# A graph network layer on one core: the selector's product in four instructions of three tiles

## The chip, the core and the metric

The kernel runs on one core of a Trainium2 chip. A core has five engines with an instruction stream each: PE (matrix products), DVE (vector), ACT (scalar), POOL (general, here the issuer of gathers) and SP (here the issuer of most plain loads). The metric is the device time of one execution in microseconds (us). The median of 16 executions of the kernel before is 4510.51 us, the lowest 4504.17, the highest 4518.46.

## The reference

There are 12500 nodes of 160 numbers (64 scalars, and 32 vectors of three components) and 400000 edges, sorted by their destination. Cut to what matters, with `a` the node attribute and the scale factors left in:

```python
h = jnp.maximum(_layernorm(x, axis=-1), 0.0)
y0 = x0 @ W_l1_0 * a * inv0
y1 = jnp.einsum('nuc,uv->nvc', x1, W_l1_1) * a[:, :, None] * inv1
w = jax.nn.silu(edge_length_embedded @ fc_W1 * ...) @ fc_W2 * ...      # 192 weights for each edge
ys0 = y0[edge_src]
ys1 = y1[edge_src]
e0 = edge_attr[:, :1]
e1 = edge_attr[:, 1:]
mid_a = w_a * ys0 * e0
mid_d = w_d * jnp.einsum('euc,ec->eu', ys1, e1) * (1.0 / math.sqrt(3.0))
mid_b = (w_b * ys0)[:, :, None] * e1[:, None, :]
mid_c = (w_c * e0)[:, :, None] * ys1
z0 = zeros.at[edge_dst].add(concatenate([mid_a, mid_d]))
z1 = zeros.at[edge_dst].add(concatenate([mid_b, mid_c]))
out0 = C_S * s0 + C_X * (z0 @ W_l2_0 * ...)
out1 = C_S * s1 + C_X * (einsum(z1, W_l2_1) * ...)
return x + concatenate([out0, out1])
```

`edge_attr` is called e4 in the kernel: its first number is `e0`, and the other three are its vector part `e1`. The product with the vector part in `mid_b` is where the change lies.

## The kernel before

**Stages.** First the node stage normalizes the nodes, multiplies them by the first weights, keeps the part `s` in `acc` on the chip and writes the part `y` to the table `y_d` in HBM. Then the edge loop runs, from about 284 us to 4443 us of the profile. Last comes a short stage that adds `acc` to `x` and writes the output. A loop for edges that are far from their window stands between; it is not entered with these inputs.

**Units of the edge loop.** An edge tile is 128 edges, one on each partition; there are 3125. A block is 4 tiles (`GT`), so there are 782 blocks. Three tiles make a window (`WT`): since the edges are sorted, their destinations are taken to lie among 32 neighbouring nodes (`WN`). Four windows are a group (`GW`) of 12 tiles (`TG`), which is 3 blocks; there are 261 groups, the last one with 5 tiles.

**What is done for a block.**
- `load(b)` issues, from POOL, one indirect DMA for each tile (L310): it takes a column of 128 node numbers from `src_sb`, in SBUF, and gathers those rows of `y_d` into `yg`. There are 10 buffers of `yg`, and loads are issued 8 blocks ahead (`AHEAD`). The edge attributes for the weights come in as `xe`, by SP.
- `hidden_pair` (L319, L324) and `weigh` (L341, L262, L263) make the edge weights `wt`, on PE and ACT.
- `products(b)` calls `multiply` on DVE: L268 multiplies the vectors of `yg` by `e1` into `tmp`, L270 reduces them to scalar products, and L271, L272, L273 and L275 write the 256 columns of `pr`. L268 is the first that needs `yg`, and so waits for the gathers.
- `sums(b)` on PE (L385) multiplies a selector by `pr` and adds the three tiles of a window in PSUM; ACT brings the result to SBUF (L390, L392).

**The selector.** `select(g)` builds, on DVE, the tile `sel` for the 12 tiles of a group: 128 partitions x 12 tiles x 4 planes x 32 nodes. Plane 3 is 1 where the edge's destination is that node (L364, from `iota` and `drel`). Planes 0 to 2 are plane 3 times the components of `e1` (L366, from `sel` and `ev`), so that one matrix product sums the scalar part and the three parts of `mid_b`. All of these operands are in SBUF. There are three buffers of `sel`.

**The end of a group.** `turn`, `linear` and `add` (L400, L409, L421) transpose the group's sums, multiply them by the last weights and place them with the help of `place` (L413, DVE); `accumulate` (L429, DVE) adds them to `acc`.

**The order.** The order of PE, ACT and DVE is written out by hand, and is kept. In turn b, DVE gets the products of block b+1, then at the last block of a group the accumulation of the group before, or at the middle block the selector of the next group:

```python
                if b + 1 < NB:
                    products(b + 1)
                if g and k == K - 1:
                    accumulate(g - 1)
                if k == 1 and g + 1 < NG:
                    select(g + 1)
                sums(b)
```

So the selector of a group is made a block or more ahead of the sums that use it. The first one is made before the loop.

Of the kernel before, what the change touches and what calls it, by code (L numbers as in the profile page):

```python
# [13 lines left out]
ALU = mybir.AluOpType  # L14
# [4 lines left out]
P = 128  # L19
# [10 lines left out]
WN = 32  # L30
WT = 3
# [10 lines left out]
def kernel(  # L42
# [19 lines left out]
    nc = tc.nc  # L62
# [214 lines left out]
    with (  # L277
# [68 lines left out]
        def e4_group(g):  # L346
            if g // EG not in ev4:
                lo, hi = g // EG * EG * TG, min((g // EG + 1) * EG * TG, TP)
                ev = ld.tile([P, EG * TG, 4], F32, name="ev")
                nc.sync.dma_start(ev[:, :hi - lo, :].rearrange("p t c -> p (t c)"), e4[:, lo * 4:hi * 4])  # L350
                ev4[g // EG] = ev
            return ev4[g // EG][:, g % EG * TG:(g % EG + 1) * TG, :]
# [5 lines left out]
        def select(g):  # L358

            ev = e4_group(g)  # L360
            lo, hi = g * TG, min((g + 1) * TG, T)
            n = hi - lo
            sel = selp.tile([P, TG, 4, WN], F32, name="sel")
            nc.vector.tensor_tensor(sel[:, :n, 3, :], iota[:, 0:WN].unsqueeze(1).to_broadcast([P, n, WN]),  # L364
                                    drel[:, lo:hi].unsqueeze(2).to_broadcast([P, n, WN]), ALU.is_equal)
            nc.vector.tensor_tensor(sel[:, :n, 0:3, :], sel[:, :n, 3:4, :].to_broadcast([P, n, 3, WN]),  # L366
                                    ev[:, :n, 1:4].unsqueeze(3).to_broadcast([P, n, 3, WN]), ALU.mult)
            sels[g] = sel

        def products(b):  # L370
# [64 lines left out]
        with order:  # L435
            for b in range(min(AHEAD, NB)):
                load(b)
            select(0)
            hidden_pair(0)
            weigh(0)  # L440
            if NB > 1:
                weigh(1)
            products(0)
            for b in range(NB):
                g, k = divmod(b, K)
                if b + AHEAD < NB:
                    load(b + AHEAD)
                if b + 2 < NB:
                    weigh(b + 2)
                if g:  # L450
                    (turn, linear, add)[k](g - 1)
# [7 lines that stand above are left out]
                if b % 4 == 0 and b + 4 < NB:  # L459
                    hidden_pair((b + 4) // 2)  # L460
            for h in ([NG - 2] if NG > 1 else []) + [NG - 1]:
                for k, stage in enumerate((turn, linear, add, accumulate)):
                    if h == NG - 1 or min(k, K - 1) > (NB - 1) % K:
                        stage(h)
# [4 lines left out]
    with (  # L469
# [10 lines left out]
        n = nc.values_load(far_i[0:1, 0:1], min_val=0, max_val=1)  # L480
        with tc.For_i(0, n, 1) as _:  # L481
            with tc.For_i(0, ZR, P) as r:
                nc.sync.dma_start(z_d[ds(r, P), :], zero)
            with tc.For_i(0, TP // GT, 1) as g:
                xe = fp.tile([FC_IN, 512], F32, name="f_xe")
                nc.sync.dma_start(xe, e16[ds(g * FC_IN, FC_IN), :])
                ev = fp.tile([P, GT, 4], F32, name="f_ev")
# [28 lines left out]
                for k in range(GT):  # L516
                    pd = fpp.tile([P, P], F32, name="f_pd")
                    nc.tensor.transpose(pd, df[:, k:k + 1].to_broadcast([P, P]), ident)
                    sel = fp.tile([P, P], F32, name="f_sel")
                    nc.vector.tensor_scalar(sel, pd, df[:, k:k + 1], None, ALU.is_equal)  # L520
                    m = fp.tile([P, ZC], F32, name="f_m")
# [87 lines left out]
```

## Time and profile before

| what | value |
|---|---|
| median of 16 executions | 4510.51 us |
| the profiled execution | 4510.26 us, of which the span from first to last instruction is 4508.4 |
| granted PE clock, mean | 0.92 |
| PE, DVE, ACT, POOL busy | 79%, 62%, 57%, 71% of the span |
| gathers, L310 on POOL | 3125 instructions, 3207.1 us busy, mean 1026 ns |
| the selector's product, L366 on DVE | 261 instructions, 353.7 us busy, mean 1355 ns |
| the selector's comparison, L364 on DVE | 261 instructions, 142.6 us busy, mean 546 ns |
| HBM | 307.62 MB read, 16.00 MB written |

The profile comes from one execution. A row such as "L366 DVE TENSOR_TENSOR sel<-sel,ev" names the line of the kernel, the engine, the operation, and what is written and read. Rows of the timeline give the start in us from the first instruction, the length in us, and in brackets the idle time of the engine ahead of it and what ended it. Consecutive DVE instructions can overlap by a little. "issue" as the end of an idle time means that no wait is seen there.

### The profile page before, as it was taken

What the parts mean: (1) busy time and instruction counts of PE and PEld (TensorE: products, weight loads), DVE (VectorE), ACT (ScalarE), POOL (GpSimd) and SP (SyncE); (2) the same over time, 40 slices, a digit from 0 to 9 for tenths busy, and PEclk for the clock granted to TensorE, in tenths of its full rate; (3) what the DMA queues carried; (4) which work ended last, traced back from release to release, by engine and by line L of the source; (5) the groups of instructions that cost most, each with busy time, mean ns of one, the idle gap of its engine ahead of it and who ended that gap; (6) DMA issues with size and microseconds to landing.
All of it is one profiled execution on the core that took longest, in us unless ns stands there. A gap on an engine that the chain in (4) does not pass through costs nothing. (4 is left out here: it accounts for less than half of the span.)

```text
span 4508.4 us, 60313 instructions
## 1 busy us (share of the span) xinstructions
PE 3541.9 (79%) x17263; PEld 2455.2 (54%) x17263; DVE 2796.5 (62%) x6412; ACT 2567.4 (57%) x9298; POOL 3215.0 (71%) x3135
## 2 busy tenths in 40 slices
PE   4887778878777878877788878877888778788773
PEld 3555555555555555555555555555555555555552
DVE  6656666666666666666666666666666666666664
ACT  1245655655565556555655555655655565555555
POOL 0037777777777777777777777777777777777773
PEclk9999998899999989899988898999999999989997
DMA  2222222222222222222222222222222222222225
GB/s 82 71 61 71 71 69 70 71 69 71 70 71 71 69 69 72 70 71 72 69 71 71 69 69 72 70 71 69 71 71 71 68 71 69 71 71 68 71 67 170
DMA packets 245943, 327.78 MB, mean 73 GB/s; under 512 B 66040, under 2 KB 195352, under 8 KB 245352
## 3 DMA queue, kind: packets, MB, share of 16 engines
q0 software_dynamic: 150000, 256.20, 21.5%
q1 hardware_dynamic: 81030, 59.43, 4.4%
q10 hardware_dynamic: 14578, 8.25, 0.6%
q8 instruction: 141, 2.31, 0.2%
q14 instruction: 194, 1.59, 0.1%
HBM read 307.62 MB, written 16.00 MB: 72 GB/s over the span
## 5 line engine op out<-in xcount | busy, mean ns | idle before, releaser
L310 POOL DMA_INDIRECT yg<-y_d,src_sb x3125 | 3207.1, 1026 | 1187.8 <-issue 914.0
L385 PE MATMUL pz<-pr,sel 128*128 128x256 f32 x6250 | 1710.4, 422 | 680.1 <-DVE pr L275 678.7
L385 PEld LDWEIGHTS pz<-pr,sel 128*128 128x128 f32 x6250 | 1246.3, 209 | 953.5 <-DVE pr L275 528.6
L268 DVE TENSOR_TENSOR tmp<-yg,ev 128x384 f32<-128x384 f32 x782 | 436.6, 558 | 1523.5 <-DMA yg<-y_d,src_sb 1520.3
L262 ACT ACTIVATE wt<-pw,ev 128x96 f32<-128x96 f32 x3125 | 808.5, 344 | 326.4 <-ACT zs L392 212.1
L390 ACT ACTIVATE zs<-pz 32x192 f32<-32x192 f32 x1042 | 337.0, 323 | 1005.5 <-PE pz L385 996.6
L341 PE MATMUL pw<-w,hT 64*128 64x192 f32 x6250 | 780.2, 371 | 0.2 <-ACT wt L263 0.2
L341 PEld LDWEIGHTS pw<-w,hT 64*128 64x128 f32 x6250 | 533.4, 201 | 393.4 <-issue 392.4
L392 ACT ACTIVATE zs<-pz 32x64 f32<-32x64 f32 x3126 | 667.6, 214 | 41.5
L270 DVE TENSOR_REDUCE tmp<-tmp 128x128 f32<-128x384 f32 x782 | 463.8, 593 | 27.1
L319 PE MATMUL px<-xe,w 32*128 32x512 f32 x782 | 338.3, 710 | 144.6 <-DVE acc L429 143.2
L273 DVE TENSOR_TENSOR pr<-wt,yg 128x384 f32<-128x384 f32 x782 | 429.1, 549 | 0.0
L324 ACT ACTIVATE hT<-px 128x512 f32<-128x512 f32 x391 | 219.3, 595 | 328.1 <-PE px L319 324.9
L263 ACT ACTIVATE wt<-pw 128x384 f32<-128x384 f32 x782 | 398.8, 510 | 0.0
L366 DVE TENSOR_TENSOR sel<-sel,ev 128x1152 f32<-128x1152 f32 (+1 forms) x261 | 353.7, 1355 | 14.2 <-DMA ev<-in_e 5.3
L271 DVE TENSOR_TENSOR pr<-wt,yg 128x256 f32<-128x256 f32 x782 | 334.1, 427 | 0.0
L272 DVE TENSOR_TENSOR pr<-wt,yg 128x256 f32<-128x256 f32 x782 | 324.7, 415 | 0.0
L409 PE MATMUL px<-wo,za 128*128 128x160 f32 x1566 | 285.6, 319 | 0.4 <-ACT za L402 0.4
L409 PEld LDWEIGHTS px<-wo,za 128*128 128x128 f32 x1566 | 222.7, 191 | 62.2 <-ACT zs L392 33.0
L319 PEld LDWEIGHTS px<-xe,w 32*128 32x128 f32 x782 | 88.2, 204 | 275.5 <-DVE acc L429 198.3
L275 DVE TENSOR_TENSOR pr<-wt,tmp 128x128 f32<-128x128 f32 x782 | 219.9, 281 | 0.0
L421 PE MATMUL px<-os,place 128*128 128x160 f32 x1044 | 212.9, 327 | 0.4 <-ACT os L411 0.4
(78 smaller groups left out, 1733.5 us busy)
## 6 DMA issues: line engine op xcount, KB each, us to landing
yg<-y_d,src_sb POOLq DMA_INDIRECT x3125
xe<-in_e SPq DMA_DIRECT2D x784, 32.0 KB
xt<-in_x SPq DMA_DIRECT2D x26, 560.0 KB
y_d<-yb SPq DMA_DIRECT2D x13, 560.0 KB
out<-xt ACTq DMA_DIRECT2D x13, 560.0 KB
ev<-in_e SPq DMA_DIRECT2D x32, 192.0 KB
src_sb<-in_src SPq DMA_DIRECT2D x1, 1568.0 KB
dst_i<-in_dst SPq DMA_DIRECT2D x1, 1568.0 KB
```

The lines of the kernel that those rows point to most:

```text
L262: nc.scalar.activation(wt[:, k, 0:96], pw[:, k, 0:96], AF.Copy, scale=ev[:, k, 0:1])
L263: nc.scalar.activation(wt[:, :n, 96:NW], pw[:, :n, 96:NW], AF.Copy)
L268: nc.vector.tensor_tensor(tmp[:, :n, 0:3, :], y1, ev[:, :n, 1:4].unsqueeze(3).to_broadcast([P, n, 3, M1]), ALU.mult)
L270: nc.vector.tensor_reduce(tmp[:, :n, 3, :], tmp[:, :n, 0:3, :].rearrange("p t c u -> p t u c"), AX.X, ALU.add)
L273: nc.vector.tensor_mul(pr[:, :n, 96:192].rearrange("p t (c u) -> p t c u", c=3), wt[:, :n, M0:96].unsqueeze(2).to_broadcast([P, n, 3, M1]) ...
L310: nc.gpsimd.indirect_dma_start(out=yg[:, k, :], out_offset=None, in_=y_d, in_offset=bass.IndirectOffsetOnAxis(ap=src_sb[:, t:t + 1], axis=0))
L319: nc.tensor.matmul(ph, w1[r, :], xe[r, :], start=True, stop=True)
L341: nc.tensor.matmul(pw[:, k, 0:NW], hT[r, o:o + P], w2[r, :], start=True, stop=True)
L366: nc.vector.tensor_tensor(sel[:, :n, 0:3, :], sel[:, :n, 3:4, :].to_broadcast([P, n, 3, WN]), ev[:, :n, 1:4].unsqueeze(3).to_broadcast([P, ...
L385: nc.tensor.matmul(pz[:, 0:PC], sels[g][:, t % TG, :, :], pr[:, k, :], start=t % WT == 0, stop=last)
L392: nc.scalar.activation(zs[:, 192 + M0 * c:192 + M0 * (c + 1)], pz[WN * c:WN * (c + 1), 192:PC], AF.Copy)
L409: nc.tensor.matmul(po[:m, :], za[:, k, :m], wo[:, k, :], start=k == 0, stop=k == 2)
```

## The change

`select` multiplies by the vector part of e4 in pieces of `WT` = 3 tiles, one window each. A group of 12 tiles takes four instructions of 128 x 288 elements in place of one of 128 x 1152; the last group, of 5 tiles, takes two. What is computed, the tiles, their buffers and the place of `select` in the order are as before.

```diff
             nc.vector.tensor_tensor(sel[:, :n, 3, :], iota[:, 0:WN].unsqueeze(1).to_broadcast([P, n, WN]),
                                     drel[:, lo:hi].unsqueeze(2).to_broadcast([P, n, WN]), ALU.is_equal)
-            nc.vector.tensor_tensor(sel[:, :n, 0:3, :], sel[:, :n, 3:4, :].to_broadcast([P, n, 3, WN]),
-                                    ev[:, :n, 1:4].unsqueeze(3).to_broadcast([P, n, 3, WN]), ALU.mult)
+            for t in range(0, n, WT):
+                m = min(WT, n - t)
+                nc.vector.tensor_tensor(sel[:, t:t + m, 0:3, :], sel[:, t:t + m, 3:4, :].to_broadcast([P, m, 3, WN]),
+                                        ev[:, t:t + m, 1:4].unsqueeze(3).to_broadcast([P, m, 3, WN]), ALU.mult)
             sels[g] = sel
```

## The prediction

> **What bounds the kernel now.** I read the page's busy shares first, then its costliest groups. The columns of a group are busy time, mean ns of one, idle time of the engine before, and what ended that idle time.
>
> ```profile
> PE 3541.9 (79%) x17263; PEld 2455.2 (54%) x17263; DVE 2796.5 (62%) x6412; ACT 2567.4 (57%) x9298; POOL 3215.0 (71%) x3135
> L310 POOL DMA_INDIRECT yg<-y_d,src_sb x3125 | 3207.1, 1026 | 1187.8 <-issue 914.0 <-DMA xe<-in_e 236.0 <-DMA yg<-y_d,src_sb 21.6
> ...
> L268 DVE TENSOR_TENSOR tmp<-yg,ev 128x384 f32<-128x384 f32 x782 | 436.6, 558 | 1523.5 <-DMA yg<-y_d,src_sb 1520.3
> ...
> L366 DVE TENSOR_TENSOR sel<-sel,ev 128x1152 f32<-128x1152 f32 (+1 forms) x261 | 353.7, 1355 | 14.2 <-DMA ev<-in_e 5.3
> ```
>
> PE has the largest busy share, yet it is not the bound. DVE waits 1520.3 us for gathers (L268), and PE waits 678.7 us for DVE's `pr`. The gathers are issued by POOL, one instruction per edge tile. Does POOL wait for anybody? The view of the waits, POOL alone, with total us, times, longest:
>
> ```profile
> POOL yg L310 <- issue: 914.0, 3000, 0.3
> POOL yg L310 <- DMA xe<-in_e: 236.0, 1, 236.0
> POOL yg L310 <- DMA yg<-y_d,src_sb: 21.6, 71, 0.3
> ```
>
> After the start-up wait of 236.0 us no pause is longer than 0.3 us, whatever name is beside it: that is POOL's fixed step between two issues. So from 283.7 us (first issue) to 4442.6 us (end of the last) POOL runs without a break, and the whole time is 283.7 + the sum of 3125 issues + a tail of 66 us. Only the length of an issue can change it. An undisturbed one takes 946 ns (the median of L310), with the step 1.25 us; the mean is 1026. The excess, 3125 x 80 ns = 250 us, is time on the path. Where does it come from? The timeline around one call of `select`, DVE rows and then POOL rows (start us, length us):
>
> ```profile
> 2012.18 0.28 DVE L275 TENSOR_TENSOR pr<-wt,tmp 128x128 f32<-128x128 f32 x1
> 2012.38 0.55 DVE L364 TENSOR_TENSOR sel<-iota,drel 128x384 f32<-128x384 f32 x1
> 2012.96 1.36 DVE L366 TENSOR_TENSOR sel<-sel,ev 128x1152 f32<-128x1152 f32 x1
> 2014.97 0.56 DVE L268 TENSOR_TENSOR tmp<-yg,ev 128x384 f32<-128x384 f32 x1 [0.65 <-DMA yg<-y_d,src_sb]
> 2015.56 0.59 DVE L270 TENSOR_REDUCE tmp<-tmp 128x128 f32<-128x384 f32 x1
> ...
> 2010.99 0.94 POOL L310 DMA_INDIRECT yg<-y_d,src_sb  x1 [0.30 <-issue]
> 2012.24 1.04 POOL L310 DMA_INDIRECT yg<-y_d,src_sb  x1 [0.30 <-issue]
> 2013.58 1.55 POOL L310 DMA_INDIRECT yg<-y_d,src_sb  x1 [0.30 <-issue]
> 2015.44 0.95 POOL L310 DMA_INDIRECT yg<-y_d,src_sb  x1 [0.30 <-issue]
> ```
>
> The issue at 2013.58 ends at 2015.13, which is 0.81 us after L366 ended (2014.32). The one at 2012.24 ends at 2013.28, 0.82 after L275 ended (2012.46). The issue at 2015.44 has its start inside L270, a reduction with one input, and is not lengthened. So some 0.135 us after its start (946 - 810 ns) an issue needs something that a DVE instruction with two SBUF inputs holds; it gets it when that instruction ends, and needs 0.81 us more. I applied this to all 3125 L310 rows: a lengthened row's end less 0.81 us falls within 30 ns of the end of a DVE instruction. By the DVE line released from: L366 145 us (one issue in almost every call of `select`, 0.56 us each), L275 31, L273 26, L271 26, L268 12, L364 7, L272 5. L366, the longest instruction of the loop, makes more than half of POOL's loss.
>
> **The change part by part.** What matters most is whether POOL gets through between two DVE instructions that follow each other at once. The trace has it, at L271 and L272 (two inputs each, the second started before the first ended):
>
> ```profile
> 2048.91 0.41 DVE L271 TENSOR_TENSOR pr<-wt,yg 128x256 f32<-128x256 f32 x1
> 2049.24 0.42 DVE L272 TENSOR_TENSOR pr<-wt,yg 128x256 f32<-128x256 f32 x1
> ...
> 2049.02 1.12 POOL L310 DMA_INDIRECT yg<-y_d,src_sb  x1 [0.30 <-issue]
> ```
>
> 2049.02 + 1.12 - 0.81 = 2049.33, the end of L271 and not of L272. In all lengthened rows of the trace no instruction ended between the point of need and the release: POOL is always let in at the first end.
>
> *Removed and added on DVE.* L366 has two sizes in the trace: 1152 elements 1358 ns, 480 elements 658 ns (its last call), so 1.042 ns per element and 158 ns fixed. A piece of 3 x 3 x 32 = 288 elements is then 458 ns. Independent instructions in a row overlap by 80 ns (L271 of 415 ns, L272 starts 335 ns later), so pieces start 378 ns apart and end at 458, 836, 1214 and 1592 ns. The four take 1592 ns against 1358: +234 ns x 260 = 61 us of DVE time. [...] The trace decides where that lies: DVE idles 0.65 us before the next L268 here, 1520.3 us in all, and L366's consumer, PE's L385, has no wait for `sel` in the list. So I cost it at nothing. Without that idle time L268 would be 0.23 us late, which delays PE's `pr` and still not POOL, whose buffers are free long before.
>
> *What POOL gains.* The point of need lies, after the start of L366: at about 0.75 us in 160 calls, 0.55 in 52, 1.20 to 1.34 in 48; in 16 rows at 0.08 POOL came first and was not held. With piece ends as above: at 0.75 held until 0.84, 0.09 us x 160 = 14 us; at 0.55 until 0.84, 0.29 x 52 = 15; of the late ones some 11 wait 0.27 for the last piece, 3 us, the others meet a seam; the early ones may now wait up to 0.37, 0 to 6 us. After a release the next need comes 1.25 us later, past the last piece. So 145 us shrink to 32 to 38: a gain of 109 us, end to end.
>
> *What moves.* POOL now arrives 0.4 us earlier in the block after `select`. In the rows above its next need was at 15.58, in L270, which holds nothing. 0.47 us earlier it is at 15.11, on the edge of L268 (held from 0.15 after its start), and the need after it at 16.36 falls into L271, 0.13 us. If it fell early into L268 it would cost up to 0.4. In the present trace that block loses 34 us in all, 0.13 per call, the other two 0.14 and, without L366, 0.15. Bounds: nothing (0.13 is already paid) or even 10 us gained, to 0.25 x 260 = 65 us lost. I take 17 us, near the low end, since three kinds of block with different phases all lose about 0.14.
>
> The L310 rows show the effect; what is held is unseen. [...]
>
> Sum: -109 + 17 = -92 us. The profiled execution took 4510.26 us (span 4508.4 and 1.9 around it), the median is 4510.51, so the sum stands against either: 4418 us.
>
> **The rivals.**
> *1 (0.79). As above*, 4418, its own range 4378 to 4458.
> *2 (0.07). No way in between the pieces:* if four instructions of one kind to one tile hand over without a seam, a need in any piece waits for the last. POOL then loses 0.234 us more per call: 260 x 0.234 = 61, 4571 us, slower. It decides if the release comes at 1592 ns and not at a piece's end; above 1358 ns the change loses. For it: pieces are alike and closer than the mixed lines of `multiply`. Against: L271, L272 and L273 are alike too, and release one by one.
> *3 (0.11). The gain is given back:* the earlier phase meets L268 (up to 0.4 us) and L271 (up to 0.3) in the next block in most calls. 0.3 x 260 = 78 lost, gain 31: 4480. For it: phases are locked, so a bad one repeats 260 times. Against: the present phases differ by block and lose alike.
> *4 (0.03). Another engine takes over, or the pieces wait for each other's end*: PE busy is 79%, and a group of 12 tiles shortens only from 15.9 to 15.5 us, so PE stays covered. With such waits the pieces start about 0.49 us apart, `select` grows 0.6 us and eats the 0.65 idle: 4505 to 4515.
>
> **How the numbers follow.** A measurement here tells about 0.2%, 9 us, from no change. Faster: 1 and nearly all of 3, 0.90; the same: 4 and a little of 3, 0.03; slower: 2, 0.07. The range takes in 1 with its unknown phase cost (up to 65 us lost, 10 gained, and the residue between 15 and 40) and half of 3: 4373 to 4470.
>
> **What would show it.** L366 with 1042 rows of about 458 ns, starts 0.38 apart; L310 still 3125 with a mean near 996 ns and pauses of 0.3; no L310 row over 1.4 us; idle before L268 still some 1450 us. A mean over 1026 proves 2; a mean near 1015, with more rows released from L268 and L271, proves 3; a pause of POOL over 0.3 us proves another bound.

## The result and the profile after

The changed kernel takes 4415.66 us (median of 8 executions, 4412.20 to 4421.21) against 4510.51 before. The ratio is 0.979, with a 95% interval of 0.9782 to 0.9798: 95 us faster. In a later set of runs, beside other experiments, it took 4406.61 against 4522.46 us, a ratio of 0.9739 (0.9723 to 0.9755): 116 us. The profiled execution after has a span of 4415.6 us at a granted PE clock of 0.92, as before. The selector's product is now line L368; lines behind it have moved by two.

The page's busy shares and the groups that answer to those shown of before:

```profile
PE 3520.6 (80%) x17263; PEld 2447.5 (55%) x17263; DVE 2850.7 (65%) x7193; ACT 2574.4 (58%) x9298; POOL 3124.1 (71%) x3135
...
L310 POOL DMA_INDIRECT yg<-y_d,src_sb x3125 | 3116.2, 997 | 1188.2 <-issue 901.7
...
L268 DVE TENSOR_TENSOR tmp<-yg,ev 128x384 f32<-128x384 f32 x782 | 436.4, 558 | 1378.4 <-DMA yg<-y_d,src_sb 1371.7
...
L368 DVE TENSOR_TENSOR sel<-sel,ev 128x288 f32<-128x288 f32 x1042 | 408.0, 453 | 14.3 <-DMA ev<-in_e 5.4
```

DVE has 781 instructions and 54 us of work more than before, and the kernel is faster. POOL has the same 3125 gathers and 91 us less work (3207.1 to 3116.2), with the same idle time (1187.8 to 1188.2). The waits of POOL say that it still runs without a break after the start (us in total, times, longest):

```profile
POOL yg L310 <- issue: 901.7, 2959, 0.3
POOL yg L310 <- DMA xe<-in_e: 236.2, 1, 236.2
POOL yg L310 <- DMA yg<-y_d,src_sb: 29.0, 95, 0.3
```

So the 91 us are the shorter issues. The timeline around one `select` shows how, DVE rows and then POOL rows (start us, length us; the four pieces are merged into one row):

```profile
2020.44 0.28 DVE L275 TENSOR_TENSOR pr<-wt,tmp 128x128 f32<-128x128 f32 x1
2020.64 0.55 DVE L364 TENSOR_TENSOR sel<-iota,drel 128x384 f32<-128x384 f32 x1
2021.22 1.56 DVE L368 TENSOR_TENSOR sel<-sel,ev 128x288 f32<-128x288 f32 x4
2023.22 0.56 DVE L268 TENSOR_TENSOR tmp<-yg,ev 128x384 f32<-128x384 f32 x1 [0.43 <-DMA yg<-y_d,src_sb]
2023.81 0.59 DVE L270 TENSOR_REDUCE tmp<-tmp 128x128 f32<-128x384 f32 x1
2024.32 0.41 DVE L271 TENSOR_TENSOR pr<-wt,yg 128x256 f32<-128x256 f32 x1
...
2020.51 1.03 POOL L310 DMA_INDIRECT yg<-y_d,src_sb  x1 [0.30 <-issue]
2021.85 1.02 POOL L310 DMA_INDIRECT yg<-y_d,src_sb  x1 [0.31 <-issue]
2023.17 0.95 POOL L310 DMA_INDIRECT yg<-y_d,src_sb  x1 [0.30 <-issue]
2024.43 1.13 POOL L310 DMA_INDIRECT yg<-y_d,src_sb  x1 [0.30 <-issue]
```

The issue at 2021.85 ends at 2022.87; less 0.81 that is 2022.06, the end of the second piece (pieces start 0.37 us apart and take 0.45, so the second ends at 2022.04). It took 1.02 us where the one in the same place took 1.55 before. The last POOL row shows the price: at 2024.43 the need falls into L271 and waits for its end at 2024.73.

The same reading of all L310 rows (excess over an undisturbed issue of about 945 ns, put down to the DVE line at whose end the row was released), in us, for six executions. The three light ones, with most of PE's work left out, come in the experiments:

| kernel | at the selector's product | at the other lines | sum | span | span less sum |
|---|---|---|---|---|---|
| before | 145.1 | 110.3 | 255.4 | 4508.4 | 4253.0 |
| changed | 28.6 | 135.4 | 164.0 | 4415.6 | 4251.6 |
| changed, later run | 42.2 | 112.4 | 154.6 | 4407.9 | 4253.3 |
| light, one piece | 170.9 | 92.8 | 263.7 | 4515.2 | 4251.5 |
| light, four pieces | 31.6 | 98.6 | 130.2 | 4382.2 | 4252.0 |
| light, twelve pieces | 27.3 | 140.2 | 167.5 | 4418.7 | 4251.2 |

The last column is constant to 2 us: the span is a fixed 4252 us plus the lengthening of POOL's issues, in all six. That accounts for the whole gain. In each of these executions the first issue of all takes 1.30 us and matches no DVE instruction; it stands under the other lines.

### The profile page after: what moved, and what is told of

It reads as the page before. It is cut to its first block, busy times and chain, and to the rows that moved or that the text cites. A ratio compares the mean times of both kernels' runs of the same rounds, so it can differ in the third digit from the quotient of the medians.

```text
span 4415.6 us, 61094 instructions
## 1 busy us (share of the span) xinstructions
PE 3520.6 (80%) x17263; PEld 2447.5 (55%) x17263; DVE 2850.7 (65%) x7193; ACT 2574.4 (58%) x9298; POOL 3124.1 (71%) x3135
## 3 DMA queue, kind: packets, MB, share of 16 engines
q8 instruction: 141, 2.31, 0.2%
## 5 line engine op out<-in xcount | busy, mean ns | idle before, releaser
L310 POOL DMA_INDIRECT yg<-y_d,src_sb x3125 | 3116.2, 997 | 1188.2 <-issue 901.7
L268 DVE TENSOR_TENSOR tmp<-yg,ev 128x384 f32<-128x384 f32 x782 | 436.4, 558 | 1378.4 <-DMA yg<-y_d,src_sb 1371.7
L270 DVE TENSOR_REDUCE tmp<-tmp 128x128 f32<-128x384 f32 x782 | 463.9, 593 | 27.1
L273 DVE TENSOR_TENSOR pr<-wt,yg 128x384 f32<-128x384 f32 x782 | 428.6, 548 | 0.0
L368 DVE TENSOR_TENSOR sel<-sel,ev 128x288 f32<-128x288 f32 x1042 | 408.0, 453 | 14.3 <-DMA ev<-in_e 5.4
L263 ACT ACTIVATE wt<-pw 128x384 f32<-128x384 f32 x782 | 399.2, 510 | 0.0
L271 DVE TENSOR_TENSOR pr<-wt,yg 128x256 f32<-128x256 f32 x782 | 335.2, 429 | 0.0
L272 DVE TENSOR_TENSOR pr<-wt,yg 128x256 f32<-128x256 f32 x782 | 324.6, 415 | 0.0
L275 DVE TENSOR_TENSOR pr<-wt,tmp 128x128 f32<-128x128 f32 x782 | 220.0, 281 | 0.0
```

Of the source, the lines that this page charges most:

```text
L263: nc.scalar.activation(wt[:, :n, 96:NW], pw[:, :n, 96:NW], AF.Copy)
L268: nc.vector.tensor_tensor(tmp[:, :n, 0:3, :], y1, ev[:, :n, 1:4].unsqueeze(3).to_broadcast([P, n, 3, M1]), ALU.mult)
L270: nc.vector.tensor_reduce(tmp[:, :n, 3, :], tmp[:, :n, 0:3, :].rearrange("p t c u -> p t u c"), AX.X, ALU.add)
L273: nc.vector.tensor_mul(pr[:, :n, 96:192].rearrange("p t (c u) -> p t c u", c=3), wt[:, :n, M0:96].unsqueeze(2).to_broadcast([P, n, 3, M1]) ...
L310: nc.gpsimd.indirect_dma_start(out=yg[:, k, :], out_offset=None, in_=y_d, in_offset=bass.IndirectOffsetOnAxis(ap=src_sb[:, t:t + 1], axis=0))
L368: nc.vector.tensor_tensor(sel[:, t:t + m, 0:3, :], sel[:, t:t + m, 3:4, :].to_broadcast([P, m, 3, WN]), ev[:, t:t + m, 1:4].unsqueeze(3).t ...
```

## The experiments

The first three groups of kernels ran on chips that granted PE a clock of 0.80 to 0.82 instead of 0.92; there the kernel before took 5450 and 5338 us. In every kernel traced there POOL stood idle ahead of L310 for 1750 to 2254 us, against 1188 in the kernel before at 0.92, so its issues alone no longer set the time. Their times can't test the theory. The rows of their traces can, since an undisturbed issue (median 946 to 949 ns) and a DVE instruction (L270, 593 ns in the mean before and with two pieces) have the same lengths there.

**Two, six and twelve pieces.** The edit is the step of the loop:

```diff
-            for t in range(0, n, WT):
-                m = min(WT, n - t)
+            for t in range(0, n, 6):
+                m = min(6, n - t)
```

and 2 or 1 in place of 6.

> Two pieces of six tiles. Theory (POOL is let in at the end of the first two-input instruction, so what counts is where in the pieces its need falls): pieces of 576 elements take 758 ns, start 678 ns apart and end at 0.76 and 1.44 us. The most frequent need, 0.75 us after the start, meets the seam and loses about 0.01 us; the needs at 0.55 lose 0.2, the late ones 0.1 to 0.24. POOL loses 20 to 35 us at this line in place of 145, and the time is 4400 to 4430 us, about that of four pieces. Rival (the loss goes with the length of one instruction): half of 145, some 72 us at this line, 4450 to 4465 us.

> Six pieces of two tiles. Theory of the seams: pieces of 192 elements take 358 ns, start 278 ns apart, ends at 0.36, 0.64, 0.91, 1.19, 1.47 and 1.75 us. Needs at 0.75 now wait 0.17 us (160 x 0.17 = 27 us), those at 0.55 wait 0.1: 30 to 40 us at this line, 4405 to 4435 us, no better than four pieces although the pieces are shorter. Rival (the loss goes with the length of one instruction): 20 to 25 us at this line, 4395 to 4408 us.

> Twelve pieces of one tile. Theory: pieces of 96 elements take 258 ns and start 178 ns apart; no need waits over 0.12 us, and some calls have two needs in their 2.2 us: 15 to 25 us at this line. DVE takes 0.6 us more per call than with four pieces, which is more than the 0.43 us that it idles before the next L268, but POOL waits for nothing of DVE's: 4395 to 4425 us. Rival (DVE's added time comes onto the path once its idle time behind the selector is used up): 0.2 to 0.4 us x 260 slower than four pieces, 4465 us or more.

Measured against the kernel before on the same chip: two pieces 1.0093 (1.0062 to 1.0125), six 1.0166 (1.0124 to 1.0207), twelve 0.9837 (0.9796 to 0.9878). Two pieces were run once more, with the same expected loss, on a second chip that again granted 0.82: 1.005 (1.0023 to 1.0078). None of the expected times came. The waits of POOL with two pieces say why:

```profile
DVE pr L271 <- ACT wt L263: 1204.1, 259, 40.5
POOL yg L310 <- DVE pr L275: 1043.1, 233, 11.7
POOL yg L310 <- issue: 847.7, 2768, 1.7
POOL yg L310 <- DMA xe<-in_e: 236.4, 1, 236.4
```

POOL now has breaks of up to 11.7 us until `multiply` is through with a block, which gives a buffer of `yg` back, and DVE in turn waits for ACT's weights. What sets the pace behind them was not followed to its end. The granted clock of PE differs too. Here are 200 us of the loop, first in the kernel before, at a granted clock of 0.92, then with two pieces here, at 0.77 (busy us of PE, PEld, DVE, ACT, POOL, with the number of instructions; granted clock; DMA share; GB/s):

```profile
2000.00:2200.00 200.00, 158.44 (x793) 109.80 (x795) 124.94 (x277) 116.99 (x426) 153.71 (x152) 0.92 0.26 71
...
2000.00:2200.00 200.00, 142.54 (x633) 100.17 (x635) 96.66 (x225) 96.74 (x348) 119.68 (x119) 0.77 0.21 56
```

POOL has 119 instructions in place of 152 in the same time. No trace of the kernel before at the low clock was kept. The rows say more than the times. With two pieces POOL lost 42.8 us at the product (42.7 in the second run), more than the 20 to 35 expected, and far from half of 145. With six it lost 15.9, less than the 30 to 40 that I expected from the phase. Since the phases differ on this chip, this doesn't separate "the phase decides" from "the length decides". In both, every row held at the product was released at the first end of a piece. With twelve pieces they were not:

```profile
385.67 2.11 DVE L368 TENSOR_TENSOR sel<-sel,ev 128x96 f32<-128x96 f32 x12
387.70 0.55 DVE L268 TENSOR_TENSOR tmp<-yg,ev 128x384 f32<-128x384 f32 x1
...
386.76 2.31 POOL L310 DMA_INDIRECT yg<-y_d,src_sb  x1 [0.30 <-issue]
```

386.76 + 2.31 - 0.81 = 388.26, the end of L268 (388.25): six pieces ended in between and POOL was not let in. 256 rows were passed over at one to six pieces, and lost 298 us. The rival of the prediction in which pieces hand over without a seam does exist, for pieces of 96 elements, though not for 192, 288 or 576.

Elsewhere a seam was missed with longer instructions too. From the run of two pieces, at L415 (a comparison of `iota` with one number per partition, which builds `place`):

```profile
400.98 0.35 DVE L415 TENSOR_SCALAR place<-iota,at 128x256 f32<-128x256 f32 x1
401.24 0.55 DVE L268 TENSOR_TENSOR tmp<-yg,ev 128x384 f32<-128x384 f32 x1
...
401.13 1.48 POOL L310 DMA_INDIRECT yg<-y_d,src_sb  x1 [1.21 <-DVE pr L275]
```

The need at 401.27 lies inside L415, which ends at 401.33, but 401.13 + 1.48 - 0.81 = 401.80 is the end of L268. Such rows number 97 with two pieces and 107 with six, and lost 52 and 57 us.

**One SBUF input.** What holds POOL up, a long instruction or one with two SBUF inputs? In the kernel before, the product is replaced by a reduction of the same size:

```diff
-            nc.vector.tensor_tensor(sel[:, :n, 0:3, :], sel[:, :n, 3:4, :].to_broadcast([P, n, 3, WN]),
-                                    ev[:, :n, 1:4].unsqueeze(3).to_broadcast([P, n, 3, WN]), ALU.mult)
+            nc.vector.tensor_reduce(sel[:, :n, 0:3, :], sel[:, :n, 3:4, :].to_broadcast([P, n, 3, WN]).unsqueeze(4),
+                                    AX.X, ALU.add)
```

> The selector's product as one instruction of the same 1152 elements, but a reduction over an axis of one, which has a single SBUF input: planes 0 to 2 become copies of plane 3, and the multiplication by e1 is left out. Theory (two SBUF inputs hold what POOL needs): an instruction of about 1.3 us that holds nothing, 0 us lost at this line, and 4385 to 4410 us with the phase given back. Rival (any long DVE instruction holds POOL up): 4500 to 4515 us as before.

> The selector's product as one instruction of the same 1152 elements with a single SBUF input (a reduction over an axis of one): planes 0 to 2 become copies of plane 3, and the multiplication by e1 is left out. Where PE is granted about 0.92: theory (two SBUF inputs hold what POOL needs) 0 us lost at this line, 4385 to 4410 us after the phase has given back 20 to 35. Rival (any long DVE instruction holds POOL up): 4500 to 4515 us. Where PE is granted about 0.80, POOL waits for buffers and no theory expects a gain in time.

> The same single-input product (the multiplication by e1 is left out) in four pieces of three tiles. It takes the number of instructions apart from what they hold: DVE has some 0.2 us more per call, about 55 us in all, and POOL loses nothing at this line either way. Theory (DVE's time is hidden in its wait for gathers): within 10 us of the single instruction with one input. Rival (more instructions cost time by themselves): 50 to 60 us slower than it.

Both runs of the single instruction were on chips with the low clock, and slower than before there: 1.018 (1.0142 to 1.0218) and 1.0175 (1.0095 to 1.0256); four pieces of it 1.0242 (1.0169 to 1.0316). The times say nothing for or against at this clock. The rows decide:

```profile
1908.41 1.35 DVE L366 TENSOR_REDUCE sel<-sel 128x1152 f32<-128x1152 f32 x1
1909.68 0.55 DVE L268 TENSOR_TENSOR tmp<-yg,ev 128x384 f32<-128x384 f32 x1
...
1909.50 0.94 POOL L310 DMA_INDIRECT yg<-y_d,src_sb  x1 [0.30 <-issue]
1910.74 0.95 POOL L310 DMA_INDIRECT yg<-y_d,src_sb  x1 [0.30 <-issue]
```

The issue at 1909.50 has its point of need, 0.135 us later, inside a DVE instruction as long as the one of before, and takes 0.94 us. In the first run 207 issues had their need inside L366 (at least 0.15 us after its start and over 0.02 us before its end), in the second 196: none took over 0.96 us, and the sum lost was under 0.1 us. In the kernel before it was 252 issues and 145 us. So it isn't the length of an instruction alone. The operation has changed too, from a product to a reduction; the next experiment keeps it.

**One of two inputs from PSUM.** The changed kernel, with L271 and L275 reading the weights where PE left them:

```diff
-        nc.scalar.activation(wt[:, :n, 96:NW], pw[:, :n, 96:NW], AF.Copy)
...
+        if all:
+            nc.scalar.activation(wt[:, :n, 96:NW], pw[:, :n, 96:NW], AF.Copy)
...
-        nc.vector.tensor_mul(pr[:, :n, 192:PC], wt[:, :n, 96:160], yg[:, :n, 0:M0])
+        w = wt if pw is None else pw
+        nc.vector.tensor_mul(pr[:, :n, 192:PC], w[:, :n, 96:160], yg[:, :n, 0:M0])
...
-        nc.vector.tensor_mul(pr[:, :n, M0:96], wt[:, :n, 160:NW], tmp[:, :n, 3, :])
+        nc.vector.tensor_mul(pr[:, :n, M0:96], w[:, :n, 160:NW], tmp[:, :n, 3, :])
```

In the edge loop `all` is False and `w` is `pw`, the tile in PSUM. L263 and its work fall away.

> The changed kernel, with L271 and L275 reading the edge weights straight from PSUM, so that they have one SBUF input each; ACT's copy of these weights (L263, 399 us busy) falls away. Theory: the 46 and 34 us that POOL loses at these two lines in the changed kernel go, some 10 to 30 come back at other lines by the phase: 4345 to 4390 us. Rivals: the operand from PSUM holds POOL up all the same, 4405 to 4425 us; PSUM is kept longer and PE's next weights come late, over 4425 us.

Again at the low clock: 1.016 (1.0086 to 1.0233). No expected time can be judged. The rows are the cleanest control of all, because operation and size are those of L271 in the changed kernel, and only one operand has moved (the line is L273 here, and the gather is L312):

```profile
2518.24 0.41 DVE L273 TENSOR_TENSOR pr<-pw,yg 128x256 f32<-128x256 f32 x1
...
2518.36 0.95 POOL L312 DMA_INDIRECT yg<-y_d,src_sb  x1 [0.30 <-issue]
```

The need at 2518.50 lies inside L273, and the issue takes 0.95 us. 146 issues had their need inside L273 by the same count, none over 0.96 us; in the changed kernel it was 267 inside L271, of which 208 were held, 46 us (the other 59 had it no later than 0.163 us after its start). So it is the second operand in SBUF that makes POOL wait for this product. It isn't the only form that does: in this run 157 issues with their need some 0.06 us before the end of L417 (the comparison that builds `place`, of one array with one number per partition) were released at its end. What in it holds POOL was not tried. In the run of two pieces, issues in the same position went past the end of this comparison to the end of L268; what tells the two apart is open. Whether this version would win at the clock of 0.92 wasn't run.

**The light kernels, on a chip that granted the kernel before 0.92.** To take PE out of the question, most of its work is left out, in the kernels with one, four and twelve pieces:

```diff
-            hT = hids[b // 2]
-            pw = p_w.tile([P, GT, 256], F32, name="pw")
+            if b < 2:
+                pws[b] = p_w.tile([P, GT, 256], F32, name="pw")
+            pw = pws[b % 2]
...
-                nc.tensor.matmul(pz[:, 0:PC], sels[g][:, t % TG, :, :], pr[:, k, :], start=t % WT == 0, stop=last)
+                if last:
+                    nc.tensor.matmul(pz[:, 0:PC], sels[g][:, t % TG, :, :], pr[:, k, :], start=True, stop=True)
...
-                if b % 4 == 0 and b + 4 < NB:
-                    hidden_pair((b + 4) // 2)
```

> The kernel before with little PE work: the edge weights come from the first two blocks only (L319, L324 and L341 run once for them, ACT still scales for every block), and L385 multiplies the last tile of each window alone. DVE's and POOL's work is whole. Theory (POOL's issues set the time, PE none of it): POOL without a break, 130 to 150 us lost at L366, 4480 to 4530 us on a chip of any clock. Rival (PE sets the time): well under 4400 us where PE is granted 0.92, and far under the 5340 to 5450 of the whole kernel where it is granted 0.80, with breaks of POOL left.

> The changed kernel with the same PE work left out as in l_one. Theory: 20 to 45 us lost at the four pieces, 80 to 115 us less than l_one. Rivals: no way in between the pieces, 40 to 70 us more than l_one; given back at other lines, less than 40 us less.

> Twelve pieces of one tile, with the same PE work left out as in l_one. First theory (let in at every piece's end): 60 to 130 us less than l_one. Theory after the run of twelve pieces in the whole kernel, where needs at the sixth piece and later were met only at the end of the next L268: POOL is not let in between pieces of 96 elements, most calls lose 0.7 us or more, and the time is 60 to 300 us more than l_one.

> The changed kernel as it is, beside the others on this chip. Where PE is granted about 0.92: 4405 to 4425 us, ratio 0.979. Where it is granted about 0.80, POOL waits for buffers that PE frees late, and what POOL saves is waited off: between the same and 2% slower than before, as with two and six pieces; POOL's loss at the pieces is still 20 to 60 us.

Measured: one piece 4509.23 us, four 4388.90, twelve 4423.11, and the whole changed kernel 4406.61 beside 4522.46 of before. With one piece PE's instructions fell from 17263 to 6085 and the time by 13 us: PE was not the bound. POOL lost 170.9 us at the product there, more than the 130 to 150 expected. Four pieces gained 120 us, a little above the 80 to 115 expected. The whole changed kernel came inside its expected 4405 to 4425 us, but its ratio of 0.9739 is a larger gain than the expected 0.979. What was expected of it at 0.80 did not come up; in the run of two pieces POOL's breaks at that clock ended with DVE's L275 (1043.1 us), and that PE frees the buffers late was not shown. The L310 rows of the light kernels, one piece and then four:

```profile
L311 POOL DMA_INDIRECT yg<-y_d,src_sb x3125 | 3215.5, 1029 | 1187.9 <-issue 937.1 <-DMA xe<-in_e 236.2 <-DMA yg<-y_d,src_sb 7.3
...
L311 POOL DMA_INDIRECT yg<-y_d,src_sb x3125 | 3082.2, 986 | 1188.2 <-issue 930.4 <-DMA xe<-in_e 236.1 <-DMA yg<-y_d,src_sb 10.1
```

133 us less POOL work, and the spans of these two executions differ by 133 us (4515.2 and 4382.2). Twelve pieces were 86 us faster than one and 34 slower than four, so the first expectation held for the time and the second did not, although its mechanism is in the trace: 69 rows were passed over at one or more seams and lost 45 us, against 256 and 298 us in the whole kernel at the low clock. Why fewer rows were passed over here is open: L268 followed the pieces with hardly any idle time in 217 of 261 calls here too. The run shows once more that PE doesn't set the time. Its PE clock in tenths over the span, after that of four pieces:

```profile
PEclk9999999999999999999999999999999999999997
...
PEclk9985555555555555555555555555555555555555
```

PE was granted half its clock nearly throughout (0.53 in the mean, against 0.99 with four pieces), and the span was still 4251 us plus POOL's loss.

## Why the prediction was right

The forecast was 4418 us, and 4415.66 was measured. The mechanism was right; that the number is right to 2 us is luck, because two errors cancelled and the same change gained 116 us in the later runs. Point by point:

- *The bound.* POOL's issues alone set the time: shown by the constant last column of the table, and by the light kernels.
- *What holds POOL.* Two SBUF inputs: shown by the reduction (no row held in 403) and by the operand from PSUM (none in 146). The comparison for `place` holds it too (157 issues in the run with the operand from PSUM), which the prediction did not see. The prediction only read it off L270. What it is that an issue needs 0.135 us after its start was not shown.
- *The way in between pieces.* Right for 288 elements: every row held at the product was released at a first end, and of the others only one, at 4193.51 us, went past an end (that of L275) to the next (that of L364). The evidence, L271 and L272, was of 256 elements; it would have misled for 96, and for the seam between L415 and L268 at the low clock.
- *What POOL gains.* Expected 32 to 38 us left at the product, measured 28.6, and 42.2 and 31.6 in the other two executions with four pieces. The pieces were a little faster than worked out: 451 ns long and 369 apart, not 458 and 378.
- *What moves.* The term that was mis-sized: 17 us given back at other lines, measured 25. The phase did what was described: L271 went from 26 to 46 us and L268 from 12 to 22, while L273 fell from 26 to 12. In the other two executions it was 2 and 6 us (112.4 against 110.3, 98.6 against 92.8; the first compares with the trace of before from the earlier runs, when that kernel was 12 us faster), so 17 lies inside a spread that no row of the trace of before could narrow. The errors of the last two terms, 6 and 8 us, cancelled.
- *DVE's 61 us at no cost.* Right. DVE grew by 54 us, and the span less POOL's loss was 4251.6 us for 4253.0 before.
- *The signs.* The L368 rows, the mean of L310 (997 ns for 996) and the pauses came as stated. One L310 row took 1.56 us, over the limit of 1.4: the one at 4193.51 us, held at L275 and L364 and not at the product. DVE's idle time before L268 was given as some 1450 us and came as 1371.7. I took off DVE's added work and forgot that a kernel that is 93 us shorter has 93 us less to idle in: 1520.3 - 54 - 93 = 1373.
- *The rivals.* No seam between pieces: refuted at this size, real at 96 elements. The gain given back: about a third of what the third rival priced (25 of 78 us), at most. Another engine in POOL's place: not at a clock of 0.92. At 0.80 to 0.82 POOL's issues did not set the time alone (1750 us and more of idle time in every trace), and there the versions with a mean issue of 989 to 1017 ns, two and six pieces among them, were 0.5 to 2.4% slower than before. The changed kernel itself wasn't run there, and why these versions cost time there is open.

## What to carry to other kernels

When the issue of indirect gathers is the bound, look at the length of its instructions against the vector engine's. Here an undisturbed issue took 946 ns, and a lengthened one ended 0.81 us after the end of a two-input vector instruction, which named the cause; the sum over all rows, 255 us, was the most that any cure of it could give, and four pieces gave 95 to 120. Cutting one instruction of 1358 ns into four of 451 helped even though it made 54 us more vector work, because the vector engine idled (1520 us for the gathers before). Moving one operand to PSUM or using a reduction with a single SBUF input took the hold away in the rows (none held in 146 and in 403); what that is worth in time was not measured where the gathers were the bound. Don't cut too finely: in the light kernels twelve pieces of 96 elements took 34 us more than four of 288. And check which engine is the bound at the clock that the chip grants: at 0.80 to 0.82 two and six pieces were 0.5 to 1.7% slower than before.

## What the runs showed that I had not expected

Pieces of 96 elements can shut POOL out over several seams, up to six pieces and the following L268 (2.31 us for an issue of 0.95), although they overlap by the same 80 ns as longer ones (251 ns each, twelve in 2.11 us). In other calls POOL was let in at once at such a seam, and in some a seam between longer instructions (L415 and L268) shut it out as well (97 rows with two pieces, 107 with six); what tells them apart is open.

The same kernel took 4510 to 4522 us on chips that granted PE 0.92 and 5338 to 5450 on chips that granted 0.80 to 0.82. There the kernel with the longest issues (twelve pieces, mean 1099 ns) was the only one faster than before, at 0.9837. In the light kernel of twelve pieces, at a granted PE clock of 0.53 but with 6085 of 17263 PE instructions, the time was still set by POOL's issues: the span less POOL's loss was 4251.2 us.
